# Softmax denominators of the third part: running sums on VectorE and GpSimd in place of products with ones

## The chip, the cores and the metric

The kernel runs on one core of a Trainium2 chip. The metric is the device time of one execution in microseconds (us); smaller is better. The engines are named as the profile names them: PE is TensorE (PEld its weight loads), DVE is VectorE, ACT is ScalarE, POOL is GpSimd, SP is the engine that issues the DMAs. A q behind a name is the engine's sequencer.

## What is computed

Two transformer layers over x of shape (2, 1024, 512), all in float32, each an attention and a feed-forward, with a layer norm ahead of each and a residual sum behind it:

```
x = x + gated_delta_attention(layernorm(x))
x = x + gelu_ffn_from_4bit_weights(layernorm(x))
x = x + latent_attention(layernorm(x))
x = x + sparse_2to4_silu_ffn(layernorm(x))
```

The change lies in the third line. With 16 heads, 1024 tokens, a head's query and key 16 wide and its value 32 wide:

```
q_latent, kv_latent = x @ wq_d, x @ wkv_d            # 64 wide each
q, k = rope(q_latent @ wq_u), rope(kv_latent @ wk_u)
v    = kv_latent @ wv_u
attn = softmax(q k^T / 4)      # per head, over all 1024 keys
out  = (attn @ v) @ wo
```

A softmax's numerators are exp(score - maximum), and its denominator is their sum over all keys. The kernel multiplies the numerators with v first and divides by the denominator afterwards.

## The kernel before

**Parts.** The program runs in parts, most of them two streams of work woven together by `weave(main, fill)`: the main stream yields a number, and as long as the sum of these numbers is positive, pieces of the fill stream are emitted between its own. The first part of the latent attention (batch element 0, the `first` stream) runs with the 4-bit feed-forward as its fill. The third part (batch element 1, `third`, lines 2074 to 2085) runs with the sparse feed-forward of batch element 0 as its fill. The order of the instructions on PE, DVE, ACT and POOL is that in which the program emits them; each engine works through its own queue in order and waits on semaphores where data or a buffer is not ready.

**The latent attention** is `Latent.run`. It makes latents, keys and values for 8 tiles of 128 tokens, and then, for each of two blocks of 512 queries, the stages `scores` (maxima of the scores) and `values`. `per_value` is what `values` yields: 3.0 in the first part, 0 in the third. With 0 the weave emits no fill, so in the third part `values` has the engines to itself. That is what the flag `alone` says.

**values** goes through 32 units: 4 groups of 4 heads, and for each group 8 tiles of 128 keys (kt 0 to 7). The pieces of a unit u are

- `weights` (lines 1557 to 1577): four products of 17 rows (16 of the key and one that carries the maximum) into two PSUM tiles `st_ps` of 128x1024, two heads each, and their exponentials by ACT into two SBUF tiles `es` of 128x1024. In the third part every third of these PSUM tiles is two single banks (`spot`), and its exponential two instructions of 512. `es` has 8 buffers in the third part (four units) and 6 in the first.
- `gather` (line 1588), one iteration later: four products of `v` with `es` into `av_ps`, 32 rows for each head, summed over the 8 key tiles. Behind the last one DVE copies `av_ps` to `oT` (line 1601).
- the denominators. In the first part (`running`), `add` (line 1628) sums `es` over the key tiles into `acc` on DVE, two adds of 128x1024 per unit, and once per group `total_run` (line 1637) multiplies `acc` with ones into `den_ps`. In the third part, `pair` (line 1603) adds the `es` of an odd key tile to those of the even one before it, in place and per head: heads 0 to 2 on POOL, head 3 on DVE. One odd iteration later `total` (line 1610) multiplies that sum with ones into `den_ps`, so there are four products for every two units, summed in PSUM over the four pairs. Behind the last pair DVE copies `den_ps` to `dn` in SBUF (line 1624).
- `divide` (line 1646): for each of four blocks of 128 queries a reciprocal on DVE and a multiply of `oT` with it. These are kept in `late` and emitted at the end of an iteration, up to three at a time.

A float32 product appears as two matmul records. The four products of a burst lie on different rows or columns of the array and run side by side, which is why eight records take about 1 us together.

After `values` the next `scores` stage takes over the same SBUF: the output weights `wo` and the rows `xl` are loaded by SP (lines 1699 and 1441) into space that `es` had.

**The loop** that sets the order is at lines 1652 to 1671; iteration u emits `weights(u)`, `gather(u - 1)`, the sums, and then the late divides.

Of the kernel before, what the change touches and what calls it, by code (L numbers as in the profile page):

```python
# [26 lines left out]
F32 = mybir.dt.float32  # L27
# [9 lines left out]
P = 128  # L37
B, T, DM = 2, 1024, 512
NT = B * T // P
TT = T // P  # L40
# [14 lines left out]
QB = 512  # L55
QT = QB // P
# [1305 lines left out]
class Latent:  # L1362
# [42 lines left out]
            nc.tensor.transpose(ps[:, gr * P : (gr + 1) * P], src[:, 4 * gr : 4 * gr + 4, :], self.core.ident)  # L1405
        nc.scalar.copy(dst, ps.rearrange("p (g t) -> p g t", g=4))

    def run(self, b, side, parked, out, per_score, per_value, running, beside=None, xT=None):

# [2 lines left out]
        core, nc, banks = self.core, self.core.nc, self.banks  # L1414
        p = core.pools(f"l_one{b}", side=side)
        self.tmp = core.pools(f"l_tmp{b}", 1, side=side)
        alone = per_value == 0
# [9 lines left out]
        two = stage("k")  # L1427
        beside = beside(lambda: two) if beside else iter(())
# [122 lines left out]
        def values(q2, oT):  # L1551

            units = [(gr, kt) for gr in range(4) for kt in range(TT)]
            es, av, den, acc = {}, {}, {}, {}
            late, count = deque(), [0]

            def weights(u):
                gr, kt = units[u]
                tiles = [spot() for _ in range(2)]
                for h4 in range(4):  # L1560
                    r = 32 * h4
                    nc.tensor.matmul(  # L1562
                        tiles[h4 // 2][h4 % 2],
                        kT[r : r + CR, gr, kt * P : (kt + 1) * P],
                        q2[r : r + CR, gr, :],
                        start=True,
                        stop=True,
                    )
                es[u] = []
                for tile in tiles:  # L1570
                    t = two.tile([P, 2, QB], F32, tag="es", bufs=8 if alone else 6, name="es")
                    if len(tile) == 3:
                        nc.scalar.activation(t.rearrange("p i q -> p (i q)"), tile[2], AF.Exp, scale=HALF**-0.5)  # L1573
                    else:
                        for i in range(2):
                            nc.scalar.activation(t[:, i, :], tile[i], AF.Exp, scale=HALF**-0.5)
                    es[u].append(t)

            def spot():


                count[0] += 1
                if alone and count[0] % 3 == 0:
                    return [banks.one("st_ps") for _ in range(2)]
                tile = banks.two("st_ps")
                return [tile[:, :QB], tile[:, QB:], tile]

            def gather(u):
                gr, kt = units[u]
                if kt == 0:  # L1590
                    av[gr] = banks.acc.tile([P, QB], F32, tag="av", name="av_ps")
                for h4 in range(4):
                    nc.tensor.matmul(  # L1593
                        av[gr][32 * h4 : 32 * h4 + 32, :],
                        v[:, kt, 4 * gr + h4, :],
                        es[u][h4 // 2][:, h4 % 2, :],
                        start=(kt == 0),
                        stop=(kt == TT - 1),
                    )
                if kt == TT - 1:  # L1600
                    nc.vector.tensor_copy(oT[:, gr, :], av.pop(gr))

            def pair(u):

                for h4 in range(4):
                    t = es[u - 1][h4 // 2][:, h4 % 2, :]
                    eng = nc.vector if alone and h4 == 3 else nc.gpsimd
                    eng.tensor_add(t, t, es[u][h4 // 2][:, h4 % 2, :])  # L1608

            def total(u):  # L1610
                gr, kt = units[u]
                if kt == 1:
                    den[gr] = banks.acc.tile([P, QB], F32, tag="den", name="den_ps")
                for h4 in range(4):
                    nc.tensor.matmul(  # L1615
                        den[gr][32 * h4 : 32 * h4 + 32, :],
                        self.ones,
                        es[u - 1][h4 // 2][:, h4 % 2, :],
                        start=(kt == 1),
                        stop=(kt == TT - 1),  # L1620
                    )
                if kt == TT - 1:
                    dn = two.tile([P, QB], F32, tag="dn", bufs=1, name="dn")
                    nc.vector.tensor_copy(dn, den.pop(gr))
                    for q in range(QT):
                        late.append(lambda q=q: divide(gr, q * P, dn, dn[:, q * P : (q + 1) * P]))

            def add(u):

                gr, kt = units[u]  # L1630
                if kt == 1:
                    acc[gr] = two.tile([P, 4, QB], F32, tag="acc", bufs=1, name="acc")
                for e in range(2) if kt else ():
                    t = acc[gr][:, 2 * e : 2 * e + 2, :]
                    nc.vector.tensor_add(t, es[u - 1][e] if kt == 1 else t, es[u][e])  # L1635

            def total_run(gr):
                den = banks.acc.tile([P, QB], F32, tag="den", name="den_ps")
                for h4 in range(4):
                    nc.tensor.matmul(  # L1640
                        den[32 * h4 : 32 * h4 + 32, :], self.ones, acc[gr][:, h4, :], start=True, stop=True
                    )
                for q in range(QT):
                    late.append(lambda q=q: divide(gr, q * P, den))

            def divide(gr, q, ps, rd=None):
                if rd is None:
                    rd = two.tile([P, P], F32, tag="rd", name="rd")
                nc.vector.reciprocal(rd, ps[:, q : q + P])
                nc.vector.tensor_mul(oT[:, gr, q : q + P], oT[:, gr, q : q + P], rd)  # L1650

            for u in range(len(units) + 3):
                if u < len(units):
                    weights(u)
                if 0 <= u - 1 < len(units):
                    gather(u - 1)
                if running:
                    if 0 <= u - 1 < len(units):
                        add(u - 1)
                    if u > TT and u % TT == 1:  # L1660
                        total_run(u // TT - 1)
                elif u % 2:
                    if u < len(units):
                        pair(u)
                    if u >= 3:
                        total(u - 2)
                yield per_value
                for _ in range(min(3, len(late))):
                    late.popleft()()
            for f in late:  # L1670
                f()
# [41 lines left out]
        for qb in range(T // QB):  # L1713
            two = stage("s")
# [6 lines left out]
            two = stage("v")  # L1721
            oT = p.tile([P, 4, QB], F32, tag="oT", name="oT1")
            yield from values(q2, oT)
        two = stage("s")
# [111 lines left out]
class Factors:  # L1836
# [29 lines left out]
    def add(self, u, t):  # L1866

        first, rest = self.core.nc.vector, self.core.nc.gpsimd
        if u[2] == "down":
            b11, b21, b22, b12, t2, t3, t4 = (t[:, i] for i in range(7))  # L1870
            first.tensor_sub(t3, b22, b12)
            rest.tensor_sub(b12, b12, b11)
            rest.tensor_sub(t2, b22, b12)
            rest.tensor_sub(t4, b21, t2)
        else:
            a11, a12, a22, s1, s2, a21, s4 = (t[:, i] for i in range(7))
            first.tensor_add(s1, a21, a22)
            rest.tensor_sub(s2, s1, a11)
            rest.tensor_sub(a21, a11, a21)
            rest.tensor_sub(s4, a12, s2)  # L1880
# [128 lines left out]
def two_layers(ctx, tc, a):  # L2009
    nc = tc.nc  # L2010
    core = Core(ctx, tc)
    pools = core.pools
    banks = Banks(ctx, tc)
# [21 lines left out]
    with tc.manual_schedule(engines={ENG.PE, ENG.DVE, ENG.Activation, ENG.Pool}):  # L2035
# [17 lines left out]


        def first():
            yield from att.run(0, "right", parks[0], parks[1], 3.4, 3.0, True, beside=factors.make)
            xs = pools("x2", side="right")
            core.hold(xs, 0)
            for n in range(TT):
                nc.sync.dma_start(out=core.x[n], in_=parks[1][n])  # L2060
            yield 2 * STEP
            xT = pools("xT_2", side="right").tile([P, KC, T], F32, name="xT2")
            yield from norms(core, banks, core.x[:TT], xT)
            done.append(xT)
# [9 lines left out]
        def third():  # L2074
            xT = pools("xT_3").tile([P, KC, T], F32, name="xT3")
            done.append(xT)
            yield from att.run(1, None, parks[0], parks[1], 3.4, 0, False, xT=xT)
            x = pools("x3").tile([P, TT, DM], F32, name="x_last")
            held.append(x)
            for n in range(TT, NT):  # L2080
                core.x[n] = x[:, n - TT, :]
                nc.sync.dma_start(out=core.x[n], in_=parks[1][n])
# [77 lines left out]
```

## Time and profile before

| | us |
|---|---|
| median of 3 runs | 3173.46 (3171.01 to 3177.64) |
| the profiled execution | 3180.04 |
| its span, first to last instruction | 3178.3 |
| mean granted clock of PE | 0.978 |

| engine | busy us | share | instructions |
|---|---|---|---|
| PE | 3087.8 | 97% | 13012 |
| DVE | 1935.2 | 61% | 3505 |
| ACT | 967.3 | 30% | 1483 |
| POOL | 735.6 | 23% | 790 |

| lines of the third part's values | engine | count | mean or median ns |
|---|---|---|---|
| 1608, adds of 128x512 | POOL | 96 | 1408 mean |
| 1608, adds of 128x512 | DVE | 32 | 1160 median |
| 1615, products with ones | PE | 256 records | 592 median |
| 1649, reciprocals | DVE | 32 | 944 median |
| 1650, multiplies | DVE | 32 | 384 median |

A line of the windows view gives start and end of a stretch, its length, each engine's busy time with the number of instructions in brackets, the granted share of PE's clock, the share of time that the DMA engines were busy, and GB/s. In the chain and the timeline a line is start, length, engine, source line and operation, in us from the start of the span; what stands in square brackets is the engine's idle time before it and what ended that.

### The profile page before, as it was taken

The page shows a single profiled execution, that of the slowest core. Times are in us where ns is not written, and L with a number is a line of the kernel's source. Part 1 is how long each engine was busy: PE and PEld are TensorE (multiplying, and loading weights), DVE is VectorE, ACT ScalarE, POOL GpSimd, SP SyncE. Part 2 cuts the span into 40 slices and gives each one's busy share as a digit, 9 for nine tenths or more (in the row PEclk, how much of TensorE's full clock was granted, in tenths as well). Part 3 has the DMA queues.
Part 4 walks back from the last instruction along what each step waited for, and adds up shares of the span by engine and source line. Part 5 has one row for each costly group of instructions (what it writes and reads, how often), then busy time and mean ns, then how long its engine had stood idle before and what let it go on. Part 6 is the DMA issues. An engine that isn't in the chain of part 4 may idle for free.

```text
span 3178.3 us, 35781 instructions
## 1 busy us (share of the span) xinstructions
PE 3087.8 (97%) x13012; PEld 1631.7 (51%) x13012; DVE 1935.2 (61%) x3505; ACT 967.3 (30%) x1483; POOL 735.6 (23%) x790
## 2 busy tenths in 40 slices
PE   7999899999999999999999999999999999999998
PEld 6778754555555554454444354346433233334547
DVE  5876753365665554357567575655675577464766
ACT  6754411122122211221354114622202710442221
POOL 3323111132222211346322121222101700440000
PEclk9999899999999999999999999999999999999999
DMA  2111234133322224236301111123000020025211
GB/s 91 38 27 29 60 101 145 34 109 91 106 87 84 92 83 162 64 124 205 112 25 58 66 48 37 47 77 119 27 30 11 9 72 14 1 70 163 70 47 50
DMA packets 194785, 229.15 MB, mean 72 GB/s; under 512 B 53745, under 2 KB 148465, under 8 KB 194097
## 3 DMA queue, kind: packets, MB, share of 16 engines
q1 hardware_dynamic: 194608, 226.86, 22.4%
q8 instruction: 103, 1.69, 0.2%
q14 instruction: 74, 0.60, 0.1%
HBM read 154.16 MB, written 72.61 MB: 71 GB/s over the span
## 4 chain that ended last, share of the span: by engine, by line
PE 83%; DVE 7%; POOL 3%; issue 2%; DMA 2%; ACT 2%; SPq 1%; DVEq 0%; POOLq 0%; ACTq 0%
PE z_ps L1018 24%; PE o_ps L201 12%; PE z_ps L1064 8%; PE u_ps L201 5%; PE g_ps L201 5%; PE st_ps L1562 5%; PE av_ps L1593 4%; PE s_ps L1504 4%; PE proj_ps L201 2%; PE small_ps L630 1%; PE wide_ps L640 1%; DVE prod L603 1%; PE wide_ps L558 1%; PE den_ps L1615 1%; PE wide_ps L397 1%
## 5 line engine op out<-in xcount | busy, mean ns | idle before, releaser
L991 ACT COPY part<-z_ps 128x512 f32<-128x512 f32 x288 | 168.5, 585 | 734.6 <-PE z_ps L1018 503.4
L1018 PE MATMUL z_ps<-xT,z_left 128*128 128x512 f32 x768 | 359.7, 598 | 0.1
L1513 DVE TENSOR_REDUCE top<-s_ps 128x2 f32<-128x1024 f32 x256 | 301.0, 1217 | 77.5 <-PE s_ps L1504 77.4
L1018 PE MATMUL z_ps<-xt,z_left 128*128 128x512 f32 x576 | 274.3, 599 | 2.2 <-issue 1.0
L1573 ACT ACTIVATE es<-st_ps 128x1024 f32<-128x1024 f32 x214 | 210.0, 1023 | 127.8 <-PE st_ps L1562 121.2
L1018 PEld LDWEIGHTS z_ps<-xT,z_left 128*128 128x128 f32 x768 | 141.2, 190 | 187.7 <-issue 162.2
L201 PE MATMUL o_ps<-w_down,h 128*128 128x512 f32 x512 | 229.5, 599 | 0.4 <-DVE part L1052 0.4
L1018 PE MATMUL z_ps<-xT,w_left 128*128 128x512 f32 x384 | 181.5, 602 | 5.0 <-DVE part L1052 2.7
L1018 PEld LDWEIGHTS z_ps<-xt,z_left 128*128 128x128 f32 x576 | 106.1, 190 | 147.1 <-issue 124.7
L1052 DVE TENSOR_TENSOR part<-z_ps,part 128x512 f32<-128x512 f32 x108 | 74.3, 689 | 174.4 <-PE z_ps L1018 168.8
L1608 POOL TENSOR_TENSOR es<-es 128x512 f32<-128x512 f32 x96 | 132.6, 1408 | 146.9 <-PE av_ps L1593 143.3
L1562 PE MATMUL st_ps<-q,kT 17*128 17x512 f32 x1024 | 161.2, 656 | 1.7 <-ACT es L1573 1.7
L1504 PE MATMUL s_ps<-kT,q 16*128 16x512 f32 x1024 | 155.5, 645 | 4.0 <-DVE top L1513 4.0
L201 PEld LDWEIGHTS o_ps<-w_down,h 128*128 128x128 f32 x512 | 95.2, 191 | 110.5 <-issue 106.2
L201 PE MATMUL proj_ps<-xT,wqkv 128*128 128x256 f32 x576 | 135.1, 388 | 10.9 <-ACT gw L427 9.6
L1593 PE MATMUL av_ps<-es,v 128*32 128x512 f32 x1024 | 140.9, 622 | 0.0
L1018 PE MATMUL z_ps<-xt,w_left 128*128 128x512 f32 x288 | 137.0, 598 | 0.7 <-DVE part L1052 0.7
L1635 DVE TENSOR_TENSOR acc<-acc,es 128x1024 f32<-128x1024 f32 x96 | 131.7, 1420 | 0.0
L1053 POOL TENSOR_TENSOR h<-h,part 128x512 f32<-128x512 f32 x48 | 66.5, 1387 | 279.8 <-DVE part L1052 279.8
L201 PEld LDWEIGHTS proj_ps<-xT,wqkv 128*128 128x128 f32 x576 | 108.1, 193 | 30.3 <-ACT gw L427 12.0
L1036 DVE TENSOR_TENSOR h<-z_ps,part 128x512 f32<-128x512 f32 x84 | 57.9, 689 | 103.1 <-PE z_ps L1018 90.0
L1161 DVE TENSOR_TENSOR x<-x,o_ps 128x512 f32<-128x512 f32 x64 | 43.9, 685 | 122.9 <-PE o_ps L201 122.8
(316 smaller groups left out, 5334.3 us busy)
## 6 DMA issues: line engine op xcount, KB each, us to landing
sums<-factor SPq DMA_DIRECT2D x24, 512.0 KB, 3.2
kept_gate<-w_left SPq DMA_DIRECT2D x12, 896.0 KB, 3.8
kept_up<-w_left SPq DMA_DIRECT2D x12, 896.0 KB, 4.1
z_left<-kept_gate SPq DMA_DIRECT2D x12, 896.0 KB, 4.6
z_left<-kept_up SPq DMA_DIRECT2D x12, 896.0 KB, 4.4
kept_down<-w_down SPq DMA_DIRECT2D x16, 512.0 KB, 3.0
wd<-kept_down SPq DMA_DIRECT2D x16, 512.0 KB, 4.1
xl<-park SPq DMA_DIRECT2D x32, 256.0 KB, 3.2
```

The costliest lines, as they stand in the source:

```text
L201: nc.tensor.matmul(ps, lhsT, rhs, start=(i == 0), stop=(i == len(pairs) - 1))
L991: self.core.nc.scalar.copy(t, src)
L1018: self.core.nc.tensor.matmul(ps, left[l][:, k, :], self.right[r][:, k, :], start=(first and k == 0), stop=(k == 1), skip_group_check=True,)
L1052: nc.vector.tensor_add(v, ps, v)
L1064: nc.tensor.matmul(ps[:, i * dm : (i + 1) * dm], left[l][:, k, i * P : (i + 1) * P], right[r][k], start=(first and i == 0 and k == 0), sto ...
L1504: nc.tensor.matmul(tiles[h4 // 2][:, h4 % 2 * 512 : h4 % 2 * 512 + 512], q1s[t][r : r + HALF, gr, :], kT[r : r + HALF, gr, j * 512 : (j + ...
L1513: nc.vector.tensor_reduce(top[:, j, h : h + 2], tiles[e].rearrange("p (i k) -> p i k", i=2), AX.X, ALU.max, negate=True)
L1562: nc.tensor.matmul(tiles[h4 // 2][h4 % 2], kT[r : r + CR, gr, kt * P : (kt + 1) * P], q2[r : r + CR, gr, :], start=True, stop=True,)
L1573: nc.scalar.activation(t.rearrange("p i q -> p (i q)"), tile[2], AF.Exp, scale=HALF**-0.5)
L1593: nc.tensor.matmul(av[gr][32 * h4 : 32 * h4 + 32, :], v[:, kt, 4 * gr + h4, :], es[u][h4 // 2][:, h4 % 2, :], start=(kt == 0), stop=(kt == ...
L1608: eng.tensor_add(t, t, es[u][h4 // 2][:, h4 % 2, :])
L1635: nc.vector.tensor_add(t, es[u - 1][e] if kt == 1 else t, es[u][e])
```

## The change

In the third part the denominators are now summed as in the first: the flag `running` is gone, as are `pair` and `total`. `add` has a second form for the third part. From the second key tile on, heads 0 and 1 are added into `acc` by one DVE add of 128x1024. On odd key tiles head 2 is a DVE add of 128x512 and head 3 a POOL add of 128x512; on even ones heads 2 and 3 are two POOL adds of 128x512. `total_run` multiplies `acc` with ones once per group, and in the third part copies `den_ps` to `dn` as `total` did. The multiply in `divide` moves to POOL in the third part. `es` has 6 buffers in both parts; `acc` has one.

```diff
-                    t = two.tile([P, 2, QB], F32, tag="es", bufs=8 if alone else 6, name="es")
+                    t = two.tile([P, 2, QB], F32, tag="es", bufs=6, name="es")
...
-            def pair(u):
-                for h4 in range(4):
-                    t = es[u - 1][h4 // 2][:, h4 % 2, :]
-                    eng = nc.vector if alone and h4 == 3 else nc.gpsimd
-                    eng.tensor_add(t, t, es[u][h4 // 2][:, h4 % 2, :])
-
-            def total(u):
...
             def add(u):
                 gr, kt = units[u]
                 if kt == 1:
                     acc[gr] = two.tile([P, 4, QB], F32, tag="acc", bufs=1, name="acc")
-                for e in range(2) if kt else ():
+                if kt and alone:
+                    n = 3 if kt % 2 else 2
+                    for eng, h0, h1 in ((nc.vector, 0, 2), (nc.vector, 2, n), (nc.gpsimd, n, 3), (nc.gpsimd, 3, 4)):
+                        if h0 < h1:
+                            t = acc[gr][:, h0:h1, :]
+                            new, old = (es[i][h0 // 2][:, h0 % 2 : h0 % 2 + h1 - h0, :] for i in (u, u - 1))
+                            eng.tensor_add(t, old if kt == 1 else t, new)
+                for e in range(2) if kt and not alone else ():
                     t = acc[gr][:, 2 * e : 2 * e + 2, :]
                     nc.vector.tensor_add(t, es[u - 1][e] if kt == 1 else t, es[u][e])
...
+                if alone:
+                    dn = two.tile([P, QB], F32, tag="dn", bufs=1, name="dn")
+                    nc.vector.tensor_copy(dn, den)
                 for q in range(QT):
-                    late.append(lambda q=q: divide(gr, q * P, den))
+                    if alone:
+                        late.append(lambda q=q: divide(gr, q * P, dn, dn[:, q * P : (q + 1) * P]))
+                    else:
+                        late.append(lambda q=q: divide(gr, q * P, den))
...
-                nc.vector.tensor_mul(oT[:, gr, q : q + P], oT[:, gr, q : q + P], rd)
+                eng = nc.gpsimd if alone else nc.vector
+                eng.tensor_mul(oT[:, gr, q : q + P], oT[:, gr, q : q + P], rd)
...
-                if running:
-                    if 0 <= u - 1 < len(units):
-                        add(u - 1)
-                    if u > TT and u % TT == 1:
-                        total_run(u // TT - 1)
-                elif u % 2:
-                    if u < len(units):
-                        pair(u)
-                    if u >= 3:
-                        total(u - 2)
+                if 0 <= u - 1 < len(units):
+                    add(u - 1)
+                if u > TT and u % TT == 1:
+                    total_run(u // TT - 1)
```

More of the change, by code (lines that the diff above doesn't have):

```diff
@@ L1406, in heads_T, with run @@
         nc.scalar.copy(dst, ps.rearrange("p (g t) -> p g t", g=4))
-    def run(self, b, side, parked, out, per_score, per_value, running, beside=None, xT=None):
+    def run(self, b, side, parked, out, per_score, per_value, beside=None, xT=None):
         core, nc, banks = self.core, self.core.nc, self.banks
@@ L1601, in gather @@
                     nc.vector.tensor_copy(oT[:, gr, :], av.pop(gr))
-            def pair(u):
-                for h4 in range(4):
-                    t = es[u - 1][h4 // 2][:, h4 % 2, :]
-                    eng = nc.vector if alone and h4 == 3 else nc.gpsimd
-                    eng.tensor_add(t, t, es[u][h4 // 2][:, h4 % 2, :])
-            def total(u):
[L1611 to L1626, printed above, removed]
             def add(u):
@@ L2055, in first @@
         def first():
-            yield from att.run(0, "right", parks[0], parks[1], 3.4, 3.0, True, beside=factors.make)
+            yield from att.run(0, "right", parks[0], parks[1], 3.4, 3.0, beside=factors.make)
             xs = pools("x2", side="right")
@@ L2076, in third @@
             done.append(xT)
-            yield from att.run(1, None, parks[0], parks[1], 3.4, 0, False, xT=xT)
+            yield from att.run(1, None, parks[0], parks[1], 3.4, 0, xT=xT)
             x = pools("x3").tile([P, TT, DM], F32, name="x_last")
```

## The prediction

> **What bounds the kernel now.** The change touches only the values of the third part, which runs with nothing woven in. I looked there first, by the busy times of the two stretches in which it runs (start and end, length, then busy us of PE, PEld, DVE, ACT, POOL, the granted clock, DMA):
>
> ```profile
> 2447.30:2539.60 92.30, 91.31 (x645) 24.56 (x644) 42.60 (x48) 64.13 (x86) 66.29 (x48) 0.94 0.00 1
> 2731.60:2825.40 93.80, 91.48 (x641) 24.71 (x641) 41.86 (x48) 65.42 (x87) 66.30 (x48) 0.95 0.00 1
> ```
>
> So 186 of 3178 us are at stake. PE is full, POOL and ACT at 70%, DVE at 46%. Next the chain of waits, two units in steady state, with start, length and what it was:
>
> ```profile
> 2492.99 1.07 PE st_ps L1562 x8
> 2494.06 1.00 PE av_ps L1593 x8
> 2495.06 1.34 PE st_ps L1562 x8
> 2496.40 1.00 PE av_ps L1593 x8
> 2497.39 0.86 PE den_ps L1615 x8
> ```
>
> TensorE sets the pace: 5.25 us per two units, 21.0 us per group of eight (the copies of dn start at 2478.27, 2499.29 and 2520.29). Third, how VectorE and GpSimd get on when both add, from the timeline. Two stretches: the 512-wide adds of this part, and the 1024-wide adds of the first part beside GpSimd's 512-wide ones.
>
> ```profile
> 2466.05 1.27 POOL L1608 TENSOR_TENSOR es<-es 128x512 f32<-128x512 f32 x1 [1.61 <-PE av_ps L1593]
> 2466.75 1.11 DVE L1608 TENSOR_TENSOR es<-es 128x512 f32<-128x512 f32 x1 [4.67 <-ACT es L1576]
> 2467.27 1.73 POOL L1608 TENSOR_TENSOR es<-es 128x512 f32<-128x512 f32 x1
> ...
> 1664.20 4.49 DVE L1635 TENSOR_TENSOR acc<-acc,es 128x1024 f32<-128x1024 f32 x2
> 1665.48 2.13 POOL L240 TENSOR_TENSOR wd<-wd 128x512 f32<-128x512 f32 x1
> 1667.69 2.16 POOL L241 TENSOR_TENSOR wd_t<-wd 128x512 f32<-128x512 f32 x1
> ```
>
> They take turns. The DVE add that starts at 2466.75 ends 0.55 us after POOL's first add, and POOL's next ends 1.14 us after that: 1.69 us for a 512 add on each. With 1024 on DVE the round is 2.21 us (POOL's starts, 1665.48 to 1667.69). Alone, the 1024 add takes 1.22, POOL's 1.27. Reciprocals (0.94) and copies out of PSUM (0.69) never grow beside POOL. Fourth, the clock at the start of the stage (same columns as the first view):
>
> ```profile
> 2447.36:2450.77 3.41, 3.20 (x20) 1.14 (x24) 0.69 (x1) 2.34 (x4) 0.00 (x0) 1.00 0.00 0
> 2450.77:2454.19 3.42, 3.42 (x16) 0.52 (x8) 1.64 (x1) 1.50 (x3) 1.74 (x2) 0.50 0.00 0
> 2454.19:2457.60 3.41, 3.41 (x20) 0.72 (x16) 0.07 (x1) 2.00 (x3) 2.43 (x2) 0.50 0.00 0
> 2457.60:2461.01 3.41, 3.41 (x20) 0.59 (x16) 0.67 (x1) 1.94 (x2) 0.75 (x1) 0.50 0.02 5
> 2461.01:2464.43 3.42, 3.42 (x28) 1.05 (x24) 1.07 (x1) 1.79 (x3) 3.42 (x3) 1.00 0.01 2
> ```
>
> The clock halves at 2450.8 and, with PE packed with st and av alone, stays halved; it returns after the window that holds the first den product (2460.1). In the second stage likewise: first den at 2745.3, clock back at 2747.7. At half clock the chain has st 2.02 and av 1.86 or 1.87, so 3.89 us a unit, and den 1.71.
>
> **Removed.** A stage has 16 bursts of den products, afterwards 4: 12 x 0.86 = 10.3 us off PE, 20.6 in both. Gone too are 48 POOL and 16 DVE adds of 512 a stage, and 16 multiplies leave DVE.
>
> **Added.** Per group (key tiles 1 to 7): seven 1024 adds and four 512 adds on DVE, ten 512 adds on POOL, and four 128x128 multiplies on POOL (0.45 each, by the rotary subtract of that shape). By lone durations (0.69 for a 512 add, as at line 957) DVE would be busy 7 x 1.22 + 4 x 0.69 + 0.69 + 0.68 + 4 x 0.94 = 16.4 us and POOL 10 x 1.27 + 4 x 0.45 = 14.5, both under the 18.5 that PE would need (4 x 4.41 + 0.86). But they take turns. An even and an odd tile together are two rounds of 2.21 and one of 1.69: 6.11 us, where PE needs 4.41. Three such pairs are 18.3 us; tile 1 adds 1.08 + 1.12 + 0.55 = 2.75.
>
> **The new wait.** acc has one buffer, so the next group's first add waits for the den product. Behind it in DVE's queue stand the copy of dn and three reciprocals: 1.0 (den with its waits) + 0.7 + 2.9 = 4.6 us in which neither engine adds. The fourth reciprocal stands ahead of tile 2's add, and POOL's fourth multiply waits for it with POOL's adds queued behind: 0.95 + 0.45 = 1.4. Period of a group by the adders: 18.3 + 2.75 + 4.6 + 1.4 = 27.0 us, against 21.0 now. es with six buffers lets ScalarE run three units ahead, not four: a unit's exp waits for the adds three units back, so PE has no way to run on.
>
> The Trainium skill, "SBUF — State Buffer", section "Who interferes with whom", says that a DVE instruction with two SBUF inputs and a GpSimd one that reads SBUF hold the shared pair for their whole length. With whole lengths a pair of tiles would be 2 x 1.22 + 0.69 + 3 x 1.27 = 6.94 us and a group about 30; the rows hand over sooner, and I go by them.
>
> **The clock.** With one den burst per group, at its end, the first group has nothing but st and av after 2450.8. By the row above I let it stay at half: 5.0 us as now, units 2 to 9 at 3.89 (31.1), den 1.71, 37.8 us in all, against 27.9 if the clock came back at 2461 (adders' pace: tile 3's exps end at 2460.2, its adds near 2462, 2 x 6.11 and den after that). Later groups lie between 27.0 (full clock, adders) and 8 x 3.89 + 1.71 = 32.8 (half clock, PE). At full clock PE would be busy 2.2 of 3.05 us a unit, 72%: the window before 2737.49 had 2.10 of 3.41, 62%, and the clock fell; the three windows from 2536 to 2539 had 0.70, 0.69, 0.82, and it held. As 72% lies between, I take the middle, 29.9. The last group has no next one's units ahead of its den: at half clock 6 x 2.02 + 7 x 1.87 + 1.0 + 1.7 = 27.9, middle 27.5.
>
> The Trainium skill, "TensorE: Matmul & The Clock Gate", section "What's actually happening", has the clock full again after one busy window of about 3.4 us. By that rule the first group would take 27.9 and, with later groups at 27.0, the change would cost some 32 us in all. The rows above show two packed windows that did not bring it back, so I don't use it.
>
> **Sum.** Stage one: 37.8 + 29.9 + 29.9 + 27.5 = 125.1, now 92.3 (2447.3 to 2539.6): +32.8. Stage two starts 0.6 slower and takes 93.6 now: 125.7, +32.1. At each end the final serial POOL adds (4.17 after the last exp) shrink, which is in the groups' terms; the multiplies leave DVE (-0.5 each), and es buffers free earlier, so the 1.4 us that PE waits for wo may go; a half clock on leaving may cost as much. I take 0. The first part's stream does not change (its es had six buffers, its sums ran on DVE): 0. No DMA is added. Total +65. The profiled execution took 3180.0, so 3245 there; it lies 6.6 above the median 3173.5, so 3239 for the median.
>
> **Rivals.**
> (a) The clock recovers as now and holds; the adders alone decide. 27.9 + 3 x 27.0 = 108.9, +16.6, and +15.9 in the second: 3206. For it: the clock held at 70%. Against: the packed st and av windows.
> (b) Half clock nearly throughout: 37.8 + 32.8 + 32.8 + 27.9 = 131.3, +39 twice: 3251; with late adders up to 3265.
> (c) Faster. If DVE and POOL fit into the gaps, PE stays the bound: -20.6, and some 2 us less at each tail: 3149. It decides as soon as a pair of tiles' adds take under 4.4 us; the sum of lone times per engine allows it, the 1.11, 1.73 and 4.49 rows speak against.
> (d) No change: gain and turns cancel, adders near 5.2 us a pair. 3173.
>
> **Numbers.** Forecast 0.50 (3222 to 3248 of its own, by how the later groups split), (a) 0.26, (b) 0.12, (c) 0.08, (d) 0.04. The range runs from (a) with adders somewhat better than the rows, +19, to (b), +89: 3192 to 3262; (c), (d) and (b)'s end lie outside. 0.2% (6 us) is about what can be told from no change: faster 0.08, same 0.04, slower 0.88.
>
> **What would show it.** Right: in these stretches PE no longer full at full clock, DVE and POOL adds long (about 2.2 and 2.1 us), dn copies 27 to 33 us apart, the clock at 0.50 through the first group, and back just after den products. Wrong: adds at 1.2 us, dn copies 18 us apart, st waiting on PE alone. The sum fails if the clock's rule isn't the one I read from two starts, or if ScalarE's exps, held by six es buffers, come later than the adders.

## The result, and the profile after

| | before | changed |
|---|---|---|
| median | 3175.44 us (4 runs, 3171.01 to 3177.64) | 3206.77 us (4 runs, 3203.48 to 3210.3) |
| profiled execution | 3180.04 | 3208.08 |
| its span | 3178.3 | 3206.4 |

The changed kernel is slower: ratio 1.0097, with a 95% interval of 1.0081 to 1.0112. That is 31 us by the medians and 28 us between the two profiled executions.

The two stretches of the third part's values, in the windows view of the changed kernel (columns as before), run from the first st product to the last copy of dn:

```profile
2446.09:2562.94 116.85, 107.32 (x548) 23.36 (x549) 83.08 (x65) 64.35 (x86) 80.59 (x52) 0.82 0.01 2
2750.92:2856.62 105.70, 94.29 (x545) 21.91 (x545) 87.96 (x64) 64.48 (x86) 86.52 (x52) 0.98 0.01 2
```

Measured in the same way (first st product to last copy of dn), the stretches were 92.4 and 93.8 us. Together they are 36 us longer; the rest of the program was 8 us shorter in this execution, to which the part on the prediction comes back. DVE went from 43 and 42 us of work to 83 and 88, POOL from 66 to 81 and 87. Part of that growth is in the length of each instruction, as the groups by line and shape show: GpSimd's adds in the kernel before (2450 to 2533 us), then the adds in the changed one (2484 to 2562 us); count, then busy us and mean ns:

```profile
L1608 POOL TENSOR_TENSOR es<-es 128x512 f32<-128x512 f32 x45 | 62.1, 1406 | 52.7 <-PE av_ps L1593 52.7
L1615 POOL TENSOR_TENSOR acc<-acc,es 128x512 f32<-128x512 f32 x27 | 51.3, 1923 | 0.7
L1615 DVE TENSOR_TENSOR acc<-acc,es 128x1024 f32<-128x1024 f32 x18 | 33.3, 1848 | 0.6
L1615 DVE TENSOR_TENSOR acc<-acc,es 128x512 f32<-128x512 f32 x9 | 15.7, 1746 | 3.5 <-POOL acc L1615 3.5
```

GpSimd's 512 adds took 1923 ns, against 1406 beside VectorE's few adds of before; VectorE's 1024 adds 1848 and its 512 adds 1746. The chain of waits passes through them:

```profile
2477.90 2.02 PE st_ps L1562 x8
2479.92 1.86 PE av_ps L1593 x8
2481.78 1.71 PE den_ps L1623 x8
2483.49 1.38 PE st_ps L1562 x8
...
2498.67 2.26 POOL acc L1615
...
2504.76 2.26 POOL acc L1615
2507.02 0.07 issue
2507.09 1.61 POOL acc L1615
2508.70 0.04 issue
2508.74 1.04 PE den_ps L1623 x2
```

Up to 2483.5 the chain is TensorE alone, at half clock. Behind that it is mostly GpSimd's adds, up to the den burst that waits for the last of them. The clock in the first stage, in windows of 3.41 us:

```profile
2446.54:2449.96 3.42, 3.21 (x24) 0.93 (x16) 0.34 (x1) 2.77 (x4) 0.00 (x0) 1.00 0.00 0
2449.96:2453.37 3.41, 3.41 (x17) 0.72 (x16) 2.89 (x2) 1.69 (x3) 1.38 (x1) 0.50 0.00 0
...
2477.27:2480.68 3.41, 3.41 (x16) 0.72 (x16) 2.42 (x3) 1.52 (x3) 0.00 (x0) 0.50 0.00 0
2480.68:2484.09 3.41, 3.41 (x20) 0.91 (x16) 0.48 (x1) 1.21 (x2) 0.00 (x0) 0.50 0.00 0
2484.09:2487.51 3.42, 3.42 (x28) 0.85 (x24) 3.39 (x5) 2.00 (x3) 1.43 (x3) 1.00 0.00 0
```

For 34 us it stayed at a half, with TensorE packed all that time by this view, and it came back behind the first den burst (2481.8). In the second stage it did not fall at the start at all. (The last groups of both stages hold another 6.8 and 3.4 us at half clock, at their end.) So the groups, from one copy of dn to the next, were:

| | first group | second | third | last | stage |
|---|---|---|---|---|---|
| before, first stage | 31.0 | 21.0 | 21.0 | 19.4 | 92.4 |
| before, second stage | 32.4 | 21.0 | 21.0 | 19.4 | 93.8 |
| changed, first stage | 37.6 | 26.2 | 26.2 | 26.9 | 116.9 |
| changed, second stage | 26.6 | 26.2 | 26.2 | 26.8 | 105.8 |

### The profile page after: what moved, and what is told of

Read it like the earlier page. It is cut to its first block, busy times and chain, and to the rows that moved or that the text cites. A ratio compares the mean times of both kernels' runs of the same rounds, so it can differ in the third digit from the quotient of the medians.

```text
span 3206.4 us, 35458 instructions
## 1 busy us (share of the span) xinstructions
PE 3098.5 (97%) x12820; PEld 1620.8 (51%) x12820; DVE 2018.7 (63%) x3529; ACT 968.1 (30%) x1483; POOL 773.7 (24%) x806
## 3 DMA queue, kind: packets, MB, share of 16 engines
q1 hardware_dynamic: 194608, 226.86, 22.4%
## 4 chain that ended last, share of the span: by engine, by line
PE 80%; DVE 8%; POOL 4%; issue 3%; DMA 2%; ACT 2%; SPq 1%; DVEq 0%; POOLq 0%; ACTq 0%
PE z_ps L1018 25%; PE o_ps L201 12%; PE z_ps L1064 8%; PE u_ps L201 5%; PE g_ps L201 5%; PE s_ps L1504 4%; PE st_ps L1562 3%; PE av_ps L1593 3%; POOL acc L1615 2%; PE proj_ps L201 2%; PE small_ps L630 1%; PE wide_ps L640 1%; DVE prod L603 1%; DVE cv L469 1%; PE wide_ps L558 1%
## 5 line engine op out<-in xcount | busy, mean ns | idle before, releaser
L1562 PE MATMUL st_ps<-q,kT 17*128 17x512 f32 x1024 | 168.4, 672 | 1.1 <-ACT es L1573 1.1
L1593 PE MATMUL av_ps<-es,v 128*32 128x512 f32 x1024 | 158.5, 634 | 7.7 <-ACT es L1573 6.2
L1615 POOL TENSOR_TENSOR acc<-acc,es 128x512 f32<-128x512 f32 x72 | 132.8, 1865 | 13.3 <-ACT es L1573 7.8
L1615 DVE TENSOR_TENSOR acc<-acc,es 128x1024 f32<-128x1024 f32 (+1 forms) x72 | 123.7, 1752 | 16.9 <-ACT es L1573 7.4
```

The source lines that it names most:

```text
L1562: nc.tensor.matmul(tiles[h4 // 2][h4 % 2], kT[r : r + CR, gr, kt * P : (kt + 1) * P], q2[r : r + CR, gr, :], start=True, stop=True,)
L1593: nc.tensor.matmul(av[gr][32 * h4 : 32 * h4 + 32, :], v[:, kt, 4 * gr + h4, :], es[u][h4 // 2][:, h4 % 2, :], start=(kt == 0), stop=(kt == ...
L1615: eng.tensor_add(t, old if kt == 1 else t, new)
```

## The experiments

**Theories.** A: the adds of VectorE and GpSimd take turns, and with the queue behind the den product that makes 26 us of a group, where TensorE would need 18.5. B: the six es buffers hold ScalarE, and through it TensorE, back. C: VectorE (or GpSimd) simply has too much to do. Beside these stands the clock: a first group that ran at half speed costs 11 us, whatever the cause of the rest.

The spacing of the copies of dn is the measure that I use most, since it leaves out the rest of the program. Where the third part's first st product begins is spread from 2441 to 2453 us over the profiled executions, a spread of the parts ahead of it, whose instructions no version here changes; a single execution's time says little below that.

### All adds on VectorE

```diff
-                if kt and alone:
+                if kt and False:
...
-                for e in range(2) if kt and not alone else ():
+                for e in range(2) if kt else ():
```

> All running adds of the third part on VectorE (two of 128x1024 a unit, as in the first part), none on GpSimd; the multiplies stay on GpSimd. Theory A (the two adding engines take turns, and that sets the pace): a group is VectorE's own work, 14 x 1.14 + 0.7 + 0.7 + 4 x 0.9 = 21 us, with the wait for den about 22, against 26.2 in the changed kernel; the time falls by 25 to 35 us, to some 3175 to 3182, though VectorE has more to do. Theory B (six es buffers instead of eight hold ScalarE back): unchanged, 3203 to 3210. Theory C (VectorE has simply too much work): slower than the changed kernel.

Measured: median 3178.06 us (10 runs), ratio to before 1.0019 (0.999 to 1.0048), so like the kernel before and 0.9% under the changed one, with half as much again for VectorE to add. Groups took 22.3 us, or 23.0 to 23.1 where the clock was at half in the den burst at their end (and 23.7 and 37.6 for the two first ones; the second of these ran at half clock). VectorE's adds, by line and shape:

```profile
L1618 DVE TENSOR_TENSOR acc<-acc,es 128x1024 f32<-128x1024 f32 x24 | 28.0, 1230 | 0.0
```

A's numbers, from 22 us, are met. B and C fall: the es buffers are six here too, and the engine that got all the work needs 1230 ns for an add that took it 1848 beside GpSimd's. Of the ten executions three took 3199 to 3204 us, at mean clocks of 0.970 and 0.971, and the others 3169 to 3183, at 0.975 to 0.981: the same kernel loses more to the clock in some of its executions than in others.

### The kernel before with six es buffers

```diff
-                    t = two.tile([P, 2, QB], F32, tag="es", bufs=8 if alone else 6, name="es")
+                    t = two.tile([P, 2, QB], F32, tag="es", bufs=6, name="es")
```

> The kernel before, with six es buffers in the third part. Theory A: the buffers are not what cost the time; within 4 us of the kernel before. Theory B: 15 us or more slower than before.

Measured: 3171.3 us, ratio 0.9977 (0.9961 to 0.9994). The buffers cost nothing (the time is 4.8 us less); the groups were even 20.7 instead of 21.0 us. Why, the runs don't tell. B falls a second time. (The changed kernel with eight was not tried.)

### One engine's adds left out

The first version leaves out GpSimd's adds in the third part, the second VectorE's (first and last pair of lines; each also feeds the den product from the sums that are left, which is not shown):

```diff
-  for eng, h0, h1 in ((nc.vector, 0, 2), (nc.vector, 2, n), (nc.gpsimd, n, 3), (nc.gpsimd, 3, 4)):
+  for eng, h0, h1 in ((nc.vector, 0, 2), (nc.vector, 2, n)):
...
+  for eng, h0, h1 in ((nc.gpsimd, n, 3), (nc.gpsimd, 3, 4)):
```

> The changed kernel without GpSimd's adds in the third part (head 3 and, on even key tiles, head 2 are left out, and heads 2 and 3 take head 1's sum, so their output is not the reference's). Theory A (turns): VectorE's adds alone take 16.4 us a group by lone durations, so TensorE sets the pace, copies of dn 18 to 19.5 us apart at full clock, VectorE's 1024 adds back at 1.22 us. If VectorE's own load is what costs the time: 24 us or more apart.

> The changed kernel without VectorE's adds in the third part (heads 0 and 1 and the odd key tiles of head 2 are left out, and all heads take head 3's sum, so the output is not the reference's). Theory A (turns): GpSimd's ten adds alone take 12.7 us a group, so TensorE sets the pace here too, copies of dn 18 to 19.5 us apart at full clock, GpSimd's adds at 1.27 us. If GpSimd is too slow for its share: 24 us or more apart.

Measured, at full clock: VectorE alone 19.5 us a group, GpSimd alone 19.1, together (the changed kernel) 26.2. The adds, by line and shape, first of the version with VectorE's alone:

```profile
L1615 DVE TENSOR_TENSOR acc<-acc,es 128x1024 f32<-128x1024 f32 x6 | 7.3, 1218 | 0.2
L1615 DVE TENSOR_TENSOR acc<-acc,es 128x512 f32<-128x512 f32 x4 | 2.7, 682 | 0.0
```

and of the one with GpSimd's alone:

```profile
L1615 POOL TENSOR_TENSOR acc<-acc,es 128x512 f32<-128x512 f32 x24 | 30.1, 1275 | 0.7
```

The same instructions took 1848, 1746 and 1923 ns when both engines added. Neither engine has too much to do; each alone leaves TensorE nearly its own pace. The loss is in the two together. These two runs show theory A by subtraction. The times, 3165.06 and 3153.45 us, are those of incomplete kernels. In the first of the two the clock fell in the third group of both stages, which took 28.7 us instead of 19.5.

### Another split

```diff
-                    n = 3 if kt % 2 else 2
+                    n = 3
```

> The changed kernel with another split: VectorE adds heads 0 to 2 on every key tile, GpSimd head 3 alone (seven adds a group instead of ten, VectorE seven of 512 instead of four). Theory A by the price of turns: three turns of 1.12 us go, three of 0.55 come, so a group falls by 1.7 us, from 26.2 to about 24.5 at full clock, between the changed kernel and the one with all adds on VectorE (22.3 to 23.1); time 3190 to 3198. If turns cost nothing and VectorE's load decides: a group grows by some 2 us.

Measured: 3208.7 us, ratio 1.0104 (1.0083 to 1.0126), groups of 26.1 us: no gain. But in the profiled execution the clock was at half in the den burst that ended every one of these groups. One group, from the timeline of VectorE, with the burst from the chain of waits:

```profile
2508.07 0.69 DVE L1628 COPY dn<-den_ps 128x512 f32<-128x512 f32 x1 [2.05 <-PE den_ps L1623]
2530.31 1.81 DVE L1615 TENSOR_TENSOR acc<-acc,es 128x1024 f32<-128x1024 f32 x2
2532.38 1.72 PE den_ps L1623 x8
2534.20 0.69 DVE L1628 COPY dn<-den_ps 128x512 f32<-128x512 f32 x1 [2.08 <-PE den_ps L1623]
```

From a copy of dn to the end of the group's last add were 24.05 us (2508.07 to 2532.12), against 25.1 in the changed kernel (2483.61 to 2508.69). So the adds became 1.0 us shorter, of the 1.7 that the price of turns had promised. From there to the next copy were 2.1 us, against 1.1 at full clock in the changed kernel: what the adds gained the clock took back. The last groups, with 30.7 us at half clock, took 29.0 us. The run speaks neither for nor against a gain at full clock; an estimate from these numbers is a group of 25.2 us.

### The gap behind the den product

```diff
-                for _ in range(min(3, len(late))):
+                for _ in range(min(1 if alone else 3, len(late))):
```

> The changed kernel, with at most one reciprocal and multiply emitted per iteration instead of three in the third part, so that one reciprocal and not three stands ahead of the next group's first add. Theory A with the queue's gap: two reciprocals of 0.89 move under GpSimd's turns, a group falls from 26.2 to about 24.4 us, the time by 10 to 14 us, to about 3194. If the gap is covered anyway: unchanged within 4 us.

In the changed kernel VectorE's queue behind the den burst looked like this (timeline):

```profile
2509.83 0.69 DVE L1628 COPY dn<-den_ps 128x512 f32<-128x512 f32 x1 [2.27 <-PE den_ps L1623]
2510.55 2.58 DVE L1638 RECIPROCAL dn<-dn 128x128 f32<-128x128 f32 x3
2513.05 2.01 DVE L1615 TENSOR_TENSOR acc<-es 128x1024 f32<-128x1024 f32 x2
```

Measured: groups of 25.4 instead of 26.2 us, so 0.8 of the 1.8 that I had expected; the reciprocals that moved only stand between later adds. Median 3210.22 us, ratio 1.0095 (1.007 to 1.0121): no gain in the time can be told. The gap is real and small.

### The multiplies back on VectorE

```diff
-                eng = nc.gpsimd if alone else nc.vector
+                eng = nc.vector
```

> The changed kernel with the multiplies back on VectorE. Theory A: GpSimd no longer waits in its queue for a reciprocal before its next add (1.3 us a group), VectorE pays four multiplies of 0.3 to 0.9 us: between -6 and +6 us against the changed kernel. If the moved multiplies are the cause of the loss: 10 us or more faster.

Measured: 3230.86 us, ratio 1.0164 (1.0134 to 1.0194), 24 us slower than the changed kernel, where I had expected nothing beyond 6. The windows view tells why (second group of the first stage, a part of the same group in the second stage, first group of the second stage):

```profile
2486.20:2517.30 31.10, 29.68 (x140) 6.09 (x140) 21.93 (x21) 15.89 (x22) 16.57 (x10) 0.62 0.00 1
2799.60:2823.50 23.90, 23.90 (x100) 4.19 (x96) 15.12 (x11) 12.47 (x18) 14.53 (x9) 0.50 0.00 1
2766.00:2792.60 26.60, 24.95 (x165) 6.33 (x168) 20.36 (x14) 19.77 (x26) 19.41 (x10) 1.00 0.01 2
```

At full clock its groups are like the changed kernel's (26.6). But the clock fell behind the den bursts, and TensorE then ran its units at half speed. The chain of waits in that second group starts with 4 us of copy, reciprocals and multiplies on VectorE, then an add and an exp for which TensorE waits, and goes on with st 2.02 and av 1.86 up to the next den burst: 31.2, 29.7, 31.4 and 31.2 us for four of its groups. From the copy to the next group's first add are 4.3 us here (2486.15 to 2490.45) and 3.2 in the changed kernel (2509.83 to 2513.05), whose clock held there. That the shorter stall is the reason was not tested.

### Bursts of products to bring the clock back

```diff
+                if alone and u in (2, 4, 6):
+                    fl = banks.acc.tile([P, QB], F32, tag="den", name="fill_ps")
+                    for h4 in range(4):
+                        nc.tensor.matmul(fl[32 * h4 : 32 * h4 + 32, :], self.ones,
+                                         es[u - 1][h4 // 2][:, h4 % 2, :], start=True, stop=True)
```

> The changed kernel with three bursts of products of es with ones in the first group of each stage (after units 1, 3 and 5, into the den bank; nobody reads them). Theory of the clock (st and av alone don't bring it back, a den burst does): where the clock falls at a stage's start it returns within 10 us, that first group takes 28 to 31 us instead of 37.6, the time falls by 5 to 10 us against the changed kernel. If the clock follows something else: first group as long as before or up to 5 us longer.

Measured: 3204.08 us, ratio 1.009 (1.0075 to 1.0106), 3 us under the changed kernel, not clear of its spread. Both first groups took 26.9 us, but in this execution the clock fell at neither start, so nothing had to be brought back: inconclusive. It fell once in the middle of a stage (third group of the second, 28.7 us).

### Towards a better version: sums over four key tiles

Sums run over four key tiles on VectorE alone, and there are two den bursts a group, accumulated in PSUM:

```diff
-                if kt == 1:
+                if kt == 1 or alone and kt == 5:
                     acc[gr] = two.tile([P, 4, QB], F32, tag="acc", bufs=1, name="acc")
...
+                for e in range(2) if kt and not (alone and kt == 4) else ():
+                    t = acc[gr][:, 2 * e : 2 * e + 2, :]
+                    nc.vector.tensor_add(t, es[u - 1][e] if kt == 1 or alone and kt == 5 else t, es[u][e])
...
+                if alone and u % TT == 5 and u < len(units):
+                    total_run(u // TT, False)      # start, no stop, no copy
```

> Sums run over four key tiles instead of eight, on VectorE alone (twelve adds of 128x1024 a group), two den bursts a group accumulated in PSUM, multiplies on GpSimd. VectorE has 12 x 1.14 + 0.7 + 0.7 + 4 x 0.9 = 18.7 us, TensorE 4 x 4.41 + 2 x 0.86 = 19.4: a group of 19.4 to 20.5 us against 21.0 before and 26.2 changed, about 10 us faster than the kernel before, 3160 to 3168. If two engines' shares are needed, slower than before.

Measured: 3186.24 us, ratio 1.0027 (1.0013 to 1.004), groups of 23.1 to 23.6 us: a miss, slower than before. In its chain of waits the first den burst of a group waits for adds that stand behind 2.58 us of reciprocals and one more of 0.87. So these were moved to key tiles 4 to 7:

```diff
-                for _ in range(min(3, len(late))):
+                for _ in range(min(u % TT > 3 if alone else 3, len(late))):
```

> The version with sums over four key tiles on VectorE, with the reciprocals moved to key tiles 4 to 7 of the next group, one per iteration, so that they no longer stand ahead of the adds that the first den burst of that group waits for. From the run with quads: 2.58 + 0.87 us of reciprocals leave that chain, a group falls from 23.1 to between 19.4 (TensorE's 4 x 4.41 + 2 x 0.86) and 20.7; time 3157 to 3168, faster than the kernel before by 0.2 to 0.6%. If reciprocals were not what held it: 23 us a group, 3180 or more.

Measured: groups of 20.1 to 20.4 us, as expected, but 3171.45 us with a ratio of 0.9988 (0.9973 to 1.0002), not told from the kernel before. In the profiled execution the clock fell at both starts and the first groups took 32.1 and 33.7 us. With two bursts that nobody reads, as in the version above but for u in (2, 3):

> The version with sums over four key tiles and late reciprocals, plus two bursts of products of es with ones in each stage (after units 1 and 2), which nobody reads. Theory of the clock: in the version without them the clock fell at both starts of the profiled execution and came back 17 to 20 us later, right behind the first den burst. With the bursts it comes back within 11 us of the stage's start wherever it falls; a first group takes 25 to 28 us instead of 32 to 34, the time falls to 3160 to 3168. If the clock follows something else: first groups of 33 to 36 us, 3172 or more.

Measured: 3166.46 us (11 runs, 3154.72 to 3173.61), ratio to the kernel before 0.9968 (0.9955 to 0.9981). This version beats both kernels, the one before by 0.3% and the changed one by 1.3%. In its profiled execution TensorE sets the pace all through a group, as the chain of waits shows:

```profile
2493.76 1.11 PE st_ps L1562 x8
2494.87 1.00 PE av_ps L1593 x8
2495.86 1.26 PE st_ps L1562 x8
2497.12 1.00 PE av_ps L1593 x8
2498.12 0.86 PE den_ps L1620 x8
```

First groups took 26.1 us in both stages. But here too the clock fell at neither start, so the bursts' own part in the gain is not shown.

## Why the prediction was right or wrong

**The direction and the adders' turns: right.** The forecast put a group at full clock at 27.0 us by the adders, with rounds of 2.21 and 1.69 us and a gap behind den; 26.2 were measured, and the versions with one engine's adds alone (19.5 and 19.1) show that it is the two together. The rival of a gain, adds that fit in the gaps, fails by the same runs. The 0.8 us between forecast and measurement lie in the pairs of key tiles. In the group that begins at 2483.6, GpSimd's adds of the three pairs ran without a break:

```profile
2491.34 17.35 POOL L1615 TENSOR_TENSOR acc<-acc,es 128x512 f32<-128x512 f32 x9
```

That is 17.35 us where the forecast had 18.3. The gap behind the last add was 4.4 us (2508.69 to 2513.05) against 4.6, and key tile 1 with the fourth reciprocal and multiply 4.5 us (2486.83 to 2491.34) against 2.75 + 1.4.

**The size: wrong, in the two steps on the clock.** The sum said +65 us and 3239, the measurement is +31 and 3207. The rival (a), the adders alone with the clock as now, said 3206. That it came so near is luck: it put both first groups at some 28 us, which took 37.6 and 26.6, the later ones at 27.0, which took 26.2 to 26.9, and the rest of the program at no change; it became 8 us shorter. Two terms of the forecast were mis-sized.

1. "Later groups ... I take the middle, 29.9" (27.5 for the last). They ran at full clock but for the end of the last one: 26.2, 26.2 and 26.9 us in the first stage and as much in the second. That term was 8.0 us too high in each stage, 16 in all. TensorE's busy share of 72% that I set between 62% (fell) and 74% (held) was no measure. By the windows view TensorE was busy 23.24 of 25.74 us in the second group, 90%. And two windows of the changed kernel with 65 and 64% kept the clock behind them:

```profile
2484.09:2509.83 25.74, 23.24 (x140) 5.13 (x133) 22.07 (x18) 15.92 (x22) 22.38 (x14) 1.00 0.00 1
...
2798.12:2801.53 3.41, 2.22 (x13) 0.40 (x14) 3.25 (x2) 1.57 (x3) 3.33 (x3) 1.00 0.00 0
2825.43:2828.84 3.41, 2.17 (x7) 0.35 (x8) 2.16 (x2) 1.02 (x1) 3.21 (x2) 1.00 0.00 0
```

The prediction's own row from 2447.36, for its part, has TensorE busy 3.20 of 3.41 us, and the clock fell behind it. The fall that I had priced exists, though: the version with the multiplies on VectorE has groups of 29.7 to 31.4 us with 20 to 24 us at half clock in each.
2. "The first group has nothing but st and av after 2450.8 ... I let it stay at half: 37.8 us". In the first stage it took 37.6, with the clock at a half from 2450.0 to 2484.1, and came back behind the first den burst. So the working of that term was right where the clock fell. But I took both stages to fall, because both had fallen before. In the second stage it did not: 26.6 instead of 38.4, 11.8 us too much. Which starts fell in the other three executions, from 3203 to 3210 us at mean clocks of 0.976 to 0.981, is not on record.

With these two, 28 of the 65 us go, and 37 stay; the stages measured +36. The rest of the program was 8 us shorter in the changed kernel's profiled execution, a term that the sum set to 0. Some of that is the same clock: between the stages the kernel before had 6.8 us at half clock, which in the changed one fell into the last group, whose 26.9 us hold it.

**The unchanged first part, the buffers, the queues.** es with six buffers is free on the kernel before (0.9977 with it); the changed kernel with eight was not tried. The claim that no more DMA is added holds: 226.86 MB on the hardware queue in both pages.

**The two rules that were weighed.** The Trainium skill's "SBUF — State Buffer", section "Who interferes with whom", with whole durations, gave a group of about 30 us; the rows' 27.0 is nearer to 26.2. (A pair of key tiles took 5.8 us, a third of the 17.35, where whole durations gave 6.94 and the rows 6.11.) The rule of its "TensorE: Matmul & The Clock Gate", section "What's actually happening", that one busy window brings the clock back, gave +32 in all, next to the measured +31, but for another reason than it says: in the first stage the clock did not come back in nine windows of packed st and av, and the total is near because the second stage never lost it and the rest of the program became shorter.

## What to carry to other kernels

Adds with two SBUF operands on VectorE and on GpSimd were not two resources here: price them as one chain of turns, and try a version that leaves one engine out, since VectorE with all the adds (22 to 23 us a group) beat both engines together (26.2). Where a stage's TensorE work is made lighter, look at the clock before counting the gain, and read from more than one execution how often it falls. A term that is on or off by chance belongs into the range as such; a middle between on and off, like the 29.9 us of the forecast, is a time that no group of the changed kernel took.

## What the runs showed of the hardware

**The clock and its grid.** In the traces of all 13 kernels, one execution each, the granted clock changes only on a grid of 3.41 us that is fixed for an execution. Of 26 starts of a values stage, it fell at 11. In ten of these the stage's first st product lay between 0.53 us ahead of an edge of that grid and 0.43 us behind it; of the 15 starts that kept the clock none did, and the nearest lay 0.65 us ahead and 0.51 us behind. (The eleventh fall, in the kernel before, came 1.1 us behind an edge, and another start at that place kept the clock.) Seven of the 13 kernels had one start of each kind. So a fall went with where the start lay in the grid rather than with the kernel; the stretch was read from these same starts, and no run moved a start to test it. In the changed kernel a fall went with 11 us more in the first group (37.6 against 26.6), in the kernel before with six buffers with 4.4 (30.7 against 26.3). Both stages of the versions with unread bursts began outside that stretch, which is why they tell nothing of the bursts.

**What brings it back.** At all 11 starts the clock returned within 3 us of the beginning of the stage's first den burst, whenever that came: after 10 us in the kernel before, 17 to 20 with sums over four key tiles, 34 with sums over eight. But a den burst is neither enough nor needed. In the version with another split, the burst of 2532.38 to 2534.10 shown above ran at half clock, and the clock stayed there:

```profile
2529.38:2532.80 3.42, 2.36 (x12) 0.55 (x16) 2.74 (x4) 1.90 (x3) 0.00 (x0) 0.50 0.00 0
2532.80:2536.21 3.41, 3.41 (x20) 0.68 (x16) 1.97 (x3) 0.06 (x1) 0.25 (x1) 0.50 0.02 5
2536.21:2539.62 3.41, 3.41 (x16) 0.55 (x12) 3.41 (x5) 1.94 (x3) 2.70 (x4) 0.50 0.00 0
...
2560.10:2563.52 3.42, 2.05 (x12) 0.60 (x16) 2.24 (x4) 0.00 (x0) 0.00 (x0) 1.00 0.31 38
```

It came back at 2560.1, ahead of the next burst (2561.47), and the second stage of that version shows the same. In the version with the multiplies on VectorE it came back at 2570.9, 2.2 us ahead of the last group's burst (2573.16), behind two av bursts in a row. What the clock goes by at half speed stays open; no run varied the rows or columns in use to test it.
